# Graph 0's attention ahead of the main loop: score matmuls moved before the transposes, with their results in the lookups' PSUM tiles

## The chip, the cores and the metric

The kernel runs on one core of one Trainium2 chip. The metric is the device time of one execution in microseconds (us); of the kernel before, three runs are given and their median is used. A profile of one further execution comes with its trace.

## What is computed

Sixteen graphs of 1,024 nodes with 128 features pass through four layers, each followed by a residual sum and a layer norm. Layer 0 is a masked attention, layer 1 an edge maximum (`relu` of a sum of two projections, maximum over the neighbours), layer 2 a two-layer perceptron over summed neighbours, layer 3 three graph convolutions over an adjacency thinned row by row ("dilation"). The change lies in layer 0:

```
v = relu(x @ Wv.T + bv);  q = relu(x @ Wq.T + bq);  k = relu(x @ Wk.T + bk)
scores = einsum('bih,bjh->bij', q, k)
h = clip(scores * mask, 0.0, CLAMP_HI) - NEG_PENALTY * (1.0 - mask)
att = softmax(h, axis=2)
out = einsum('bij,bjh->bih', att, v)
x = layernorm(x + out)
```

## The kernel before, in words

**Stages.** After the constants are set up, `layers_012` runs layers 0 to 2 of all graphs together with the dilation. Its main loop is a written order of slots (`slot`, under `tc.manual_schedule`): each slot does one group of layer 1's lookups (matmuls into `pg`, L779, and the maximum on VectorE, L831), and a planner (`advance`) fits the generators of the other work between them, among them the attention of graph b+1. Graph 0's attention cannot hide there, since layer 1 of graph 0 needs its result. So it runs ahead of the loop, by itself. Layer 3 follows after the loop.

**A graph's attention** is two generators that yield where the planner may pause them. `scores(b)` loads the rows of the adjacency, transposes X, makes `qT`, `kT` and `v`, and then goes through eight row blocks t of 128 rows. For each it makes `off` on ScalarE (L320, one buffer: 1 minus the mask), and for each half of 512 columns a score matmul into a PSUM bank `psc` (L329) and a second one that adds the penalty (L330); VectorE clamps the half into `e` and keeps its maximum (L332, `e` has two buffers); `top` joins the two maxima (L336); ScalarE takes the exponential in place and its row sum `total` (L339). `attend(b)` takes one row block's `e`: eight transposes on TensorE in two groups `pe` of four (L367), two copies on ScalarE into `eT` (L370, one buffer), eight products `pav` with `v` in two groups (L377), the reciprocal of the sum (L380), the scaled sum with X into `y` (L381), and the first statistics of the layer norm (L265). After row block 7 the norm's factors are made on GpSimd (L219 to L228), ScalarE writes the normed X (L270), and `scores` goes on with transposes (L278) and the two projections `q` and `p` (L286) that layer 1 starts from.

**PSUM.** `pe`, `pav` and, before the change, `psc` take turns in two banks (`shared`, tag "shared", two buffers). The tag "wide" has two tiles of two banks each; only the lookups' `pg` uses it. The main loop is the only place where `pg` is made.

**Order.** Ahead of the loop a scheduler orders the instructions, from the order in which the program makes them. That order is a loop over t (from L841 on): `front` (`scores(0)`) is run until row block t's `e` is made, and then `back` (`attend(0)`) until it asks for row block t+1. `happened` is a dictionary of marks, by which the generators wait for each other. Each engine has one list of instructions, in the order that results.

Of the kernel before, what the change touches and what calls it, by code (L numbers as in the profile page):

```python
# [29 lines left out]
F32 = mybir.dt.float32  # L30
# [10 lines left out]
P = 128  # L41
T = N // P
# [29 lines left out]
def tile_graph_layers(ctx: ExitStack, tc, a, out):  # L72
# [7 lines left out]
    psum = None  # L80
# [9 lines left out]
    psum = setup.enter_context(tc.tile_pool(name="psum0", bufs=2, space=PSUM))  # L90
# [60 lines left out]
    def four(v):  # L151
        return v.unsqueeze(1).to_broadcast([3, 4, P])
# [83 lines left out]
    def layers_012():  # L236
# [3 lines left out]
        psum = psums.enter_context(tc.tile_pool(name="psumA", bufs=1, space=PSUM))  # L240
# [11 lines left out]
        happened, streams, made = {}, [], []  # L252

        def ask(engine, cost, take=False, give=False, same=False, delay=0.5, after=None, third=False, urgent=False):
            return engine, cost, take, give or urgent and None, 0 if same else delay, after, third

        def shared(name):
            return psum.tile([P, 512], F32, tag="shared", name=name, bufs=2)
# [14 lines left out]
        def columns_of(dst, src, first=0.5):  # L273
            for h in range(2):
                yield ask("PE", 0.44, take=True, delay=0.5 if h else first)
                p = shared("ptr")
                for t in range(4):
                    nc.tensor.transpose(p[:, t * P:(t + 1) * P], src[:, 4 * h + t, :], ident)  # L278
                yield ask("A", 0.59, give=True, same=True)
                nc.scalar.copy(dst[:, halves[h]], p)  # L280

        def product_of(lhsT, rhs, dst, func, bias, delay=0.5):
            for h, s in enumerate(halves):
                yield ask("PE", 0.86, take=True, delay=0.5 if h else delay)
                p = shared("pp")
                nc.tensor.matmul(p, lhsT, rhs[:, s], start=True, stop=True)  # L286
                yield ask("A", 0.6, give=True, same=True)
                if bias is None:
                    nc.scalar.copy(dst[:, s], p)  # L289
                else:  # L290
                    nc.scalar.activation(dst[:, s], p, func, bias=bias)

        def scores(b):

            if b > 1:
                yield ask("Pool", 0, after=("p", b - 1))
            if b > 2:
                yield ask("Pool", 0, after=("rest", b - 3))
            load_rows(b)
            xT = w4.tile([P, N], F32, name="xT")  # L300
            yield from columns_of(xT, X[b])
            qT = w4.tile([P, N], F32, name="qT")
            yield from product_of(WqT, xT, qT, AF.Relu, bq)
            kT = w4.tile([P, N], F32, name="kT")
            yield from product_of(WkT, xT, kT, AF.Relu, bk)
            v = values[b] = w4.tile([P, T, D], F32, name="v")
            for h in range(2):
                yield ask("PE", 1.1, take=True)
                pv = shared("pv").rearrange("p (t d) -> p t d", d=D)
                nc.tensor.matmul(pv, ones_b[:3, :], four(bv3), start=True, stop=False)  # L310
                for t in range(4):
                    nc.tensor.matmul(pv[:, t, :], xT[:, (4 * h + t) * P:(4 * h + t + 1) * P], WvT,
                                     start=False, stop=(t == 3))
                yield ask("A", 0.6, give=True, same=True)
                nc.scalar.activation(v[:, 4 * h:4 * h + 4, :], pv, AF.Relu)
            for t in range(T):

                yield ask("A", 1.05)
                off = w4.tile([P, N], BF, name="off", tag="pen")
                nc.scalar.activation(off, An[b][:, t, :], AF.Identity, bias=ones[:, 0:1], scale=-1.0)  # L320
                if t > 1:
                    yield ask("PE", 0, same=True, after=("back", b, t - 2))
                e = w4.tile([P, N], F32, name="e", bufs=2)

                tops = small.tile([P, 2], F32, name="tops")
                for h, s in enumerate(halves):
                    yield ask("PE", 1.07, take=True)
                    psc = shared("psc")
                    nc.tensor.matmul(psc, qT[:, t * P:(t + 1) * P], kT[:, s], start=True, stop=False)  # L329
                    nc.tensor.matmul(psc, penalty, off[:, s], start=False, stop=True)  # L330
                    yield ask("V", 0.66, give=True)
                    nc.vector.tensor_scalar(e[:, s], psc, CLAMP_HI, None, op0=ALU.min, op1=ALU.max,  # L332
                                            accum_out=tops[:, h:h + 1])
                yield ask("V", 0.1, same=True)
                top = small.tile([P, 1], F32, name="top")
                nc.vector.tensor_scalar(top, tops[:, 0:1], tops[:, 1:2], -1.0, op0=ALU.max, op1=ALU.mult)  # L336
                yield ask("A", 1.1)
                total = small.tile([P, 1], F32, name="total")
                nc.scalar.activation(e, e, AF.Exp, bias=top, accum_out=total)  # L339
                exps[b, t] = e, total  # L340
                happened["e", b, t] = now
            yield ask("A", 0.01, after=("X1", b), delay=0.5)
            xT = w4.tile([P, N], F32, name="xT1", tag="xT")
            yield from columns_of(xT, X[b])
            q = w4.tile([P, NP * PS], F32, name="q", bufs=2)
            nc.gpsimd.memset(q[:, N:], LOWEST)
            yield from product_of(W01[:, 1, :], xT, q[:, :N], None, None)
            qs[b] = q
            happened["q", b] = now
            if b > 1:  # L350
                yield ask("A", 0, same=True, after=("y1", b - 2))
            p = ps[b] = w4.tile([P, N], F32, name="p", bufs=2)
            yield from product_of(Wd, xT, p, AF.Identity, b01)
            happened["p", b] = now

        def attend(b):
            for t in range(T):
                yield ask("PE", 0.01, after=("e", b, t))
                if t == 0:
                    y = w4.tile([P, T, D], F32, name="y0", tag="xT")  # L360
                e, total = exps.pop((b, t))
                eT = w4.tile([P, T, P], F32, name="eT")
                for h in range(2):
                    yield ask("PE", 0.44, take=True, same=(h == 0))
                    p = shared("pe")
                    for c in range(4):
                        nc.tensor.transpose(p[:, c * P:(c + 1) * P],  # L367
                                            e[:, (4 * h + c) * P:(4 * h + c + 1) * P], ident)
                    yield ask("A", 0.59, give=True, same=True)
                    nc.scalar.copy(eT[:, 4 * h:4 * h + 4, :].rearrange("p c i -> p (c i)"), p)  # L370
                happened["back", b, t] = now
                for h in range(2):
                    yield ask("PE", 0.9, take=(h == 0))
                    if h == 0:
                        pav = shared("pav")[:, :D]
                    for c in range(4 * h, 4 * h + 4):
                        nc.tensor.matmul(pav, eT[:, c, :], values[b][:, c, :], start=(c == 0), stop=(c == T - 1))  # L377
                yield ask("V", 0.4, give=True)
                share = small.tile([P, 1], F32, name="share")
                nc.vector.reciprocal(share, total)  # L380
                nc.vector.scalar_tensor_tensor(y[:, t, :], pav, share, X[b][:, t, :], op0=ALU.mult, op1=ALU.add)  # L381
            yield from norm(X[b], y)
            happened["X1", b] = now
# [305 lines left out]
        def load_rows(b):  # L689
            An[b] = apool.tile([P, T, N], F8, name="An", bufs=3)  # L690
            nc.gpsimd.dma_start(out=An[b], in_=adj[b].rearrange("(t p) m -> p t m", p=P))
# [146 lines left out]
        for at in range(2):  # L838
            load_columns(at)
        front, back = scores(0), attend(0)  # L840
        for t in range(T):  # L841
            while ("e", 0, t) not in happened:
                next(front)
            for what in back:
                if what[5] == ("e", 0, t + 1):
                    break
        for _ in front:
            pass
        first = tables_of(0)
# [18 lines left out]
        psum = ctx.enter_context(tc.tile_pool(name="psum", bufs=2, space=PSUM))  # L868
# [301 lines left out]
```

## Time and profile before

| | us |
|---|---|
| median of three runs | 6616.69 |
| the three runs | 6604.93, 6616.69, 6620.51 |
| the profiled execution | 6613.2 |
| its span, first to last instruction | 6611.5 |
| graph 0's row blocks: start of the first transposes to the last L265 | 45.34 to 114.31 |
| start of the transposes of the eight row blocks | 45.34, 54.47, 63.92, 73.58, 81.59, 91.44, 101.09, 108.99 |
| first transpose of layer 1's table (L760) | 128.39 |

Times in the trace count from the first instruction. The profiled execution takes 1.7 us more than its span and lies 3.5 us below the median of the three runs, inside their spread of 15.6 us. Engines are PE (TensorE; PEld its weight loads), DVE (VectorE), ACT (ScalarE), POOL (GpSimd), SP (SyncE). "PEclk" is the share of TensorE's full clock that it was granted. In a line of the timeline the first number is the start, the second the time until the group's last end, and the bracket the idle time of that engine before it and what ended it.

### The profile page before, as it was taken

The numbers are of one execution on the slowest core, as the hardware profiler recorded it, in microseconds if no ns is written. First come the engines' busy times: TensorE is split into PE (matmuls) and PEld (weight loads), VectorE is DVE, ScalarE is ACT, GpSimd is POOL, SyncE is SP. The second block draws the span as 40 slices with busy tenths as digits, with TensorE's granted clock in tenths as the row PEclk, the third lists the DMA queues.
The fourth block names the chain that finished last, engine by engine and source line by source line (L and its number), as shares of the span: only waits on it lengthen the run. The fifth ranks groups of instructions, "written<-read, shape, count | busy, mean of one in ns | idle before, by whom it ended". The sixth has DMA issues, their size and how long they took to land. (4 is left out here: it accounts for less than half of the span.)

```text
span 6611.5 us, 85916 instructions
## 1 busy us (share of the span) xinstructions
PE 5697.7 (86%) x27306; PEld 2883.8 (44%) x27306; DVE 5317.7 (80%) x8130; ACT 3733.9 (56%) x6537; POOL 3844.7 (58%) x11285
## 2 busy tenths in 40 slices
PE   6989898989898989899888898888888768787986
PEld 3434344444444444444444444444443345555643
DVE  3989899999999999999999999999998834444453
ACT  4656566666666666666666656666655523333841
POOL 2675767676767776766666676767676511110126
PEclk8989898989898989898989899999987779888997
DMA  5121212121212121212112212121110156563635
GB/s 37 14 27 22 30 24 36 20 27 26 28 28 27 27 27 26 28 26 31 28 29 30 27 26 27 26 27 28 25 25 9 32 93 120 105 124 102 230 128 166
DMA packets 478381, 317.02 MB, mean 48 GB/s; under 512 B 301162, under 2 KB 429668, under 8 KB 473828
## 3 DMA queue, kind: packets, MB, share of 16 engines
q0 software_dynamic: 105648, 84.20, 14.6%
q1 hardware_dynamic: 367600, 226.13, 11.7%
q8 instruction: 214, 3.51, 0.2%
q10 hardware_dynamic: 4676, 1.19, 0.1%
q14 instruction: 243, 1.99, 0.1%
HBM read 412.71 MB, written 117.18 MB: 80 GB/s over the span
## 5 line engine op out<-in xcount | busy, mean ns | idle before, releaser
L831 DVE TENSOR_TENSOR best<-best,pg 128x1024 f32<-128x1024 f32 x2720 | 3234.4, 1210 | 309.0 <-PE pg L779 300.5
L749 ACT ACTIVATE hot<-pm,one_less 128x512 fp32r<-128x512 f32 x2752 | 1882.3, 688 | 1115.1 <-PE pm L748 1102.9
L779 PE MATMUL pg<-hot,high 64*128 64x512 f32 x5504 | 1479.1, 534 | 453.6 <-DVE best L831 417.8
L779 PE MATMUL pg<-hot,low 64*128 64x512 f32 x5504 | 1173.3, 423 | 0.0
L748 PE MATMUL pm<-AT,lit 120*128 120x512 fp8e4 x2752 | 1143.8, 416 | 9.3 <-ACT hot L749 6.2
L779 PEld LDWEIGHTS pg<-hot,high 64*128 64x128 f32 x5504 | 547.9, 196 | 1265.1 <-DVE best L831 792.4
L616 POOL TENSOR_SCALAR sc<-low_counts,half_mask,rest 16x1 f32<-16x1 f32 x992 | 435.7, 439 | 399.6 <-DVE rest L603 305.8
L779 PEld LDWEIGHTS pg<-hot,low 64*128 64x128 f32 x5504 | 573.4, 205 | 0.0
L748 PEld LDWEIGHTS <-lit 120*128 120x128 fp8e4 x2752 | 274.5, 100 | 624.8 <-issue 560.8
L621 POOL TENSOR_SCALAR sc<-sc 16x1 f32<-16x1 f32 x992 | 430.1, 434 | 105.0
L770 ACT CAST low<-pt 128x256 fp32r<-128x256 f32 x688 | 255.6, 371 | 396.3 <-PE pt L768 392.1
L980 POOL TENSOR_TENSOR length<-length,mhalf 128x8 f32<-128x8 f32 x48 | 78.9, 1644 | 571.7 <-DVE length L979 571.7
L618 POOL TENSOR_SCALAR sc<-sc 16x1 f32<-16x1 f32 x992 | 341.8, 345 | 107.7
L624 POOL TENSOR_SCALAR last_rank<-V,sc 16x31 f32<-16x31 bf16 (+30 forms) x992 | 387.1, 390 | 0.0
L623 POOL TENSOR_SCALAR hit<-V,sc 16x31 bf16<-16x31 bf16 (+30 forms) x992 | 372.5, 376 | 0.0
L768 PE MATMUL pt<-high,less 128*128 128x256 f32 x688 | 303.2, 441 | 66.3 <-ACT high L763 58.9
L467 DVE TENSOR_TENSOR sub<-sub,q 128x24 f32<-128x24 f32 (+11 forms) x768 | 306.6, 400 | 24.6 <-ACT q L289 10.5
L619 POOL TENSOR_SCALAR sc<-sc 16x1 f32<-16x1 f32 x992 | 270.1, 272 | 83.3
L937 ACT CAST m<-near 128x1024 fp32r<-128x1024 fp8e4 x256 | 253.3, 1044 | 112.7 <-DVE near L906 59.8
L760 PE MATMUL pt<-ident,sub 128*128 128x128 f32 x1376 | 293.9, 298 | 24.7 <-ACT hot L749 22.0
L377 PE MATMUL pav<-v,eT 128*128 128x128 f32 x2048 | 307.6, 296 | 2.1 <-ACT eT L370 2.1
L617 POOL TENSOR_SCALAR sc<-sc 16x1 f32<-16x1 f32 x992 | 256.6, 259 | 86.6
(258 smaller groups left out, 9495.7 us busy)
## 6 DMA issues: line engine op xcount, KB each, us to landing
removed<-gone SPq DMA_DIRECT2D x128, 256.0 KB
An<-in_adj_dram POOLq DMA_DIRECT2D x16, 1024.0 KB, 15.1
E<-in_adj_dram POOLq DMA_DIRECT2D x128, 128.0 KB, 6.8
gone_all<-removed POOLq DMA_DIRECT2D x64, 256.0 KB, 12.1
near<-in_adjT_dram POOLq DMA_DIRECT2D x16, 1024.0 KB, 17.3
h<-x SPq DMA_DIRECT2D x32, 512.0 KB
kept<-near SPq DMA_DIRECT2D x16, 1024.0 KB
share<-share SPq DMA_DIRECT2D x32, 512.0 KB
```

Source lines behind the costliest of these rows:

```text
L377: nc.tensor.matmul(pav, eT[:, c, :], values[b][:, c, :], start=(c == 0), stop=(c == T - 1))
L467: nc.vector.tensor_max(sub[:, :n_g, n:2 * n], sub[:, :n_g, 0:n], qg[:, 2 * g0:2 * g0 + n_g, k:k + 1].to_broadcast([P, n_g, n]))
L616: gp.tensor_scalar(half, mine, half_mask[:, m], rest[:, n:n + 1], op0=ALU.mult, op1=ALU.add)
L618: gp.tensor_scalar(sf, half, 5.5, sf, op0=ALU.is_gt, op1=ALU.mult)
L621: gp.tensor_scalar(to, at, sf, none, op0=ALU.subtract, op1=ALU.subtract)
L623: gp.tensor_scalar(hit[:, n, n + 1:], V[:, n, n + 1:], at, None, op0=ALU.is_equal)
L624: gp.tensor_scalar(last[:, n + 1:], V[:, n, n + 1:], to, None, op0=ALU.is_le)
L748: nc.tensor.matmul(pm, lit[:, r, :], AT[b * (T + 1) + c][:, halves[h]], start=True, stop=True)
L749: nc.scalar.activation(hots[s][:, halves[h]], pm, AF.Relu, bias=one_less)
L768: nc.tensor.matmul(pt, less, high, start=False, stop=True, skip_group_check=True)
L779: nc.tensor.matmul(pg[:, a], part[rows, at * P:(at + 1) * P], hots[s][rows, halves[h]], start=(k == 0), stop=(k == 1))
L831: nc.vector.tensor_max(own, own, pg)
```

## The change

The loop over t runs `attend` one row block later than `scores`: `scores(0)` makes row block t+1 before `attend(0)` takes row block t, and a ninth turn takes the last. Until the mark `planned` is set, ahead of the main loop, `psc` is no longer a bank of the pair "shared": each half takes a "wide" tile of two banks, and uses the bank of its own half. The first half's tiles and the second half's thus take turns in the two "wide" tiles, so each half has one bank. In the main loop `psc` is taken as before.

```
@@ -325,7 +325,10 @@
                 tops = small.tile([P, 2], F32, name="tops")
                 for h, s in enumerate(halves):
                     yield ask("PE", 1.07, take=True)
-                    psc = shared("psc")
+                    if "planned" in happened:
+                        psc = shared("psc")
+                    else:
+                        psc = psum.tile([P, 2, 512], F32, tag="wide", name="psc", bufs=2)[:, h]
                     nc.tensor.matmul(psc, qT[:, t * P:(t + 1) * P], kT[:, s], start=True, stop=False)
                     nc.tensor.matmul(psc, penalty, off[:, s], start=False, stop=True)
                     yield ask("V", 0.66, give=True)
@@ -838,12 +841,14 @@
         for at in range(2):
             load_columns(at)
         front, back = scores(0), attend(0)
-        for t in range(T):
-            while ("e", 0, t) not in happened:
+        for t in range(T + 1):
+            while t < T and ("e", 0, t) not in happened:
                 next(front)
-            for what in back:
-                if what[5] == ("e", 0, t + 1):
-                    break
+            if t:
+                for what in back:
+                    if what[5] == ("e", 0, t):
+                        break
+        happened["planned"] = 0
         for _ in front:
             pass
```

## The prediction

> **What bounds the kernel now.** I read the page first, then the stretch of graph 0's attention: a table of windows, its waits, the timeline of one row block. The page:
>
> ```profile
> span 6611.5 us, 85916 instructions
> PE 5697.7 (86%) x27306; PEld 2883.8 (44%) x27306; DVE 5317.7 (80%) x8130; ACT 3733.9 (56%) x6537; POOL 3844.7 (58%) x11285
> PEclk8989898989898989898989899999987779888997
> ```
>
> No engine is full over the span, but that is a mean over stages. The change touches one stage, 45 to 114 us of 6611.5, so 1% of the span; the whole question is what happens there and whether the rest simply starts earlier. Windows (stretch, its length, each engine's busy us, then granted clock, DMA share, GB/s):
>
> ```profile
> core 0: us, PE busy (x) PEld busy (x) DVE busy (x) ACT busy (x) POOL busy (x), PEclk, DMA share, GB/s
> 63.90:73.50 9.60, 6.93 (x30) 5.02 (x30) 2.41 (x8) 3.33 (x5) 0.00 (x0) 0.82 0.00 0
> 73.50:81.60 8.10, 5.30 (x31) 3.52 (x31) 2.45 (x9) 3.37 (x6) 0.00 (x0) 1.00 0.00 0
> 129.00:200.00 71.00, 63.54 (x319) 31.06 (x319) 53.31 (x85) 49.81 (x92) 48.77 (x174) 0.95 0.04 5
> ```
>
> The first two rows are one row block each. The busy times add up to hardly more than the length (5.30 + 2.45 + 3.37 = 11.1 of 8.10 us), where the main loop (last row) has 167 us of PE, DVE and ACT in 71: in the attention the engines work by turns. The same row block takes 9.6 or 8.1 us with the granted clock, 0.82 or 1.00. DMA moves nothing there. The waits of the stretch 41 to 119 us (engine and line, whom it waited for, us in total, times, longest) say who stands for whom:
>
> ```profile
> DVE y L381 <- PE pav L377: 35.2, 8, 4.9
> ACT off L320 <- PE psc L330: 30.0, 6, 5.7
> DVE e L332 <- PE psc L330: 21.3, 15, 15.7
> PE pe L367 <- ACT e L339: 19.7, 8, 2.7
> ```
>
> TensorE waits 2.4 us per row block for the exponential before it may transpose; all others wait for TensorE. One row block at full clock:
>
> ```profile
> 73.58 1.09 PE L367 MATMUL pe<-ident,e 128*128 128x128 f32 x8 [2.43 <-ACT e L339]
> 74.32 1.07 ACT L370 COPY eT<-pe 128x512 f32<-128x512 f32 x2 [0.80 <-PE pe L367]
> 74.96 2.05 PE L377 MATMUL pav<-v,eT 128*128 128x128 f32 x16 [0.29 <-ACT eT L370]
> 76.85 1.02 PE L329 MATMUL psc<-kT,qT 128*128 128x512 f32 x2
> 77.05 0.35 DVE L381 SCALAR_TENSOR_TENSOR y<-pav,share,X 128x128 f32<-128x128 f32 x1 [3.33 <-PE pav L377]
> 77.71 0.38 PE L330 MATMUL psc<-off,penalty 128*128 128x512 bf16 x1
> 77.92 1.02 PE L329 MATMUL psc<-kT,qT 128*128 128x512 f32 x2
> 78.78 0.38 PE L330 MATMUL psc<-off,penalty 128*128 128x512 bf16 x1
> 79.20 0.69 DVE L332 TENSOR_SCALAR_CACHE_REDUCE e<-psc 128x512 f32<-128x512 f32 x1 [0.38 <-PE psc L330]
> 79.26 1.15 ACT L320 ACTIVATE off<-An,ones 128x1024 bf16<-128x1024 fp8e4 x1 [3.87 <-PE psc L330]
> 79.93 0.21 DVE L336 TENSOR_SCALAR top<-tops 128x1 f32<-128x1 f32 x1
> 80.31 1.13 ACT L339 ACTIVATE e<-e,top 128x1024 f32<-128x1024 f32 x1
> 81.59 0.66 PE L367 MATMUL pe<-ident,e 128*128 128x128 f32 x4 [2.43 <-ACT e L339]
> ```
>
> Read it as one chain: transposes, copy, products, the next row block's scores, clamp, maximum, exponential, transposes again. From 73.58 to 81.59 nothing overlaps it. From the first transposes (45.34) to the eighth (108.99) that makes 63.65 / 7 = 9.09 us per row block.
>
> [...]by windows of 1 us the clock is 0.50 from 38.7 to 48.7 us, after TensorE had stood idle from 36 us on, and again in 55.7 to 58.6, 65.9 to 69.1, 82.9 to 86.1, 93.0 to 96.3 and 110.5 to 113.2; 24 to 36 us, without a gap, is at 1.00. So the idle 2.4 us per row block costs twice. [...]before, five results per row block share two banks.
>
> **The change, part by part.** *No instruction is added or taken away.* With both programs built, GpSimd's and SyncE's instructions stand in the same order, so no DMA is moved past another. TensorE's order differs over one run of 154 instructions, VectorE's over 43, ScalarE's over 24, all inside the eight row blocks; from the layer norm on, the order is the same. `psc` leaves the pair "shared" for 16 tiles, an even number, so the later banks fall as before; `pg` first needs the "wide" tiles long after. These parts cost nothing.
>
> *The moved order.* TensorE, for row block k: 4+4 transposes(k), first score half of k+2, first four products(k), its penalty, second score half of k+2, last four products(k), its penalty. ScalarE: off(k+2), first copy(k), exponential(k+1), second copy(k). VectorE: first clamp of k+1, y(k-1), second clamp of k+1, statistics, top(k+1), reciprocal(k+1). I count from S, the start of the second penalty of row block k+1, all steps from the timeline above, at full clock:
> - off(k+2) has one buffer and waits for this penalty: S+0.48 (78.78 to 79.26), and the next on ScalarE 1.05 later (79.26 to 80.31): S+1.53. This is the step with a new queue: the first copy(k) stands behind off(k+2) though its transposes are ready at S+0.95 (0.21 penalty, 0.74 from transposes to copy), and the products wait for that.
> - first copy(k) S+1.53, products may start 0.64 later (74.32 to 74.96): S+2.17. TensorE until then: penalty 0.21, transposes at most 1.09, score half 0.86 (76.85 to 77.71): S+2.16. Both come together.
> - four products 0.945 (half of 74.96 to 76.85), penalty 0.21, score half 0.86: S+4.18. Last four products need the second copy, which stands behind exponential(k+1): y at S+0.20 takes 0.35, clamp to top 0.73, statistics 0.29, 0.25 from top to the exponential (107.44 to 107.69 in another row block): S+1.82, while ScalarE is free at S+2.07; the exponential with its sum takes 1.22, the copy starts at S+3.29, and products may start at S+3.93, before 4.18. Hidden by 0.25 us; beyond that every delay of it counts.
> - last four products 0.945: next S at S+5.13.
> So 5.13 us per row block, TensorE busy nearly throughout (sum 1.09 + 1.72 + 0.42 + 1.89 = 5.12), against 8.0 at full clock before: 2.9 us from overlap, and on average 1.1 from the clock that no longer falls.
>
> *Start.* Penalty of row block 0 at 41.83 and its first clamp until 43.14 stay. Score halves of row block 1 then take twice 0.86 at half clock: 43.15 to 44.87, and on. The clock changes seen lie on a grid of 3.4 us (38.7, 48.7, so one at 45.3); [...]I take full clock from there: second half done at 45.95, S0 = 46.16. If it comes only at 48.7, about 1.0 us is lost. *End.* S6 = 46.16 + 6 x 5.13 = 76.94. Then no off and no scores are left: copies at +0.95 and +1.49, exponential(7) +2.03 to +3.25, products(6) to +3.48, transposes(7), copy +4.22, products +4.86 to +6.75, y +6.95, statistics +7.33: 84.3. Before: 114.31. **Gain 30.0 us.** What is late next is the GpSimd norm and the half-clock projections up to 128.39, unchanged.
>
> *Does it reach the end?* The order after is the same, the DMA that runs at 1.1 of its share up to 60 us (adjacency, E) ends before 84 too, and nothing waits for the clock on the wall. I take the shift whole: 6613.2 - 30.0 = 6583.2 for the profiled execution (1.7 us outside its span kept), and 6616.69 - 30.0 = **6586.7** for the median, 0.45%. Unknown costs: late clock +1.0; handoffs in the new order, not in the trace before, from 0 (a gain is excluded, since TensorE's 5.1 binds) to 0.4 per row block, the margin of the exponential plus as much again: 0 to 2.4, taken at 0. The median itself moves by about 8 us, half the runs' spread.
>
> **Rivals.**
> 1. *The clock still falls in part.* [...]windows with 57% kept full clock before (96.7 to 100.1), which speaks against. Were half of the rows at half rate (2 x 4.9 = 9.8 us), the mean is 7.5 and the gain 30.0 - 6 x 2.35 = 16: 6601. Were all of them, the start, six cycles and the end give about 118 us against 114.31: slightly lost, 6620.
> 2. *The main loop loses it (slower).* The mean clock 0.904 means some 19% of 6611 / 3.41 = 1,939 windows at half rate, about 370. The earlier start shifts the loop on that grid; a window that turns cold costs at most half, 1.7 us. From 18 more cold windows on the kernel is slower than before; 30 more give 6616.7 - 30 + 51 = 6638. Against it: three runs that start anywhere on the grid differ by 15.6 us, nine windows.
> 3. *The change doesn't do what it says.* Each half has one bank, not two; were the clamp late, scores would wait. The clamp of k+1's first half is read before S, the second by S+1.2, the scores want them at S+1.3 and S+3.3: free. A wrong order is excluded by the built programs.
>
> **How the numbers follow.** Forecast 0.83; rival 1 0.12, of which most lies within the bound; rival 2 0.04; rival 3 0.01. About 0.3%, 20 us, is what a measurement of this kernel can tell from no change. Gain 26.6 to 30.0 and 8 us of the median up and down give 6579 to 6598; widened to 6574 and 6602 to take in rival 1's half. Faster 0.84, same 0.12, slower 0.04.
>
> **What would show it.** Right: transposes of successive row blocks 5.1 us apart; clock 1.00 from about 45 to 84 us; last L265 near 84; first L760 near 98; later differences of the same size. Wrong: waits of the products for the copies over 0.3 us per row block (ScalarE's order binds), clock 0.50 in the stretch, or a main loop that is longer than before by ten us or more.

## The result and the profile after

| | before | after |
|---|---|---|
| median | 6616.69 (five runs, 6604.93 to 6620.51) | 6580.25 (five runs, 6577.91 to 6583.07) |
| ratio | | 0.9953 [0.994, 0.9965] |
| profiled execution, and its span | 6613.2, 6611.5 | 6583.07, 6581.4 |
| mean granted clock over the span | 0.904 | 0.906 |
| first transposes of the eight row blocks | 45.34 ... 108.99 | 47.17, 52.32, 57.43, 62.54, 67.65, 72.76, 77.87, 81.09 |
| last L265 of graph 0 | 114.31 | 84.90 |
| first transpose of layer 1's table | 128.39 (L760) | 98.98 (L763) |

The kernel is 36.4 us faster by its medians, against 30.0 forecast, and 30.1 us faster by its two profiled spans. Of these 30.1 us, 29.4 are there at the first table transpose, ahead of the main loop. Behind it the lead of one profile over another wanders by several us (last table of the next section), so the close agreement of 30.1 with 29.4 is in part chance. In the changed file the lines move by three: L367 is L370, L377 is L380, L381 is L384.

The page hardly changes, as one per cent of the span can't show in it:

```profile
span 6581.4 us, 85782 instructions
PE 5669.1 (86%) x27177; PEld 2870.4 (44%) x27306; DVE 5314.9 (81%) x8130; ACT 3735.2 (57%) x6537; POOL 3854.6 (59%) x11285
PEclk9899899999898989898989899999998788888998
```

The 129 fewer PE instructions than before are records that this trace lacks: e5, the same kernel, has 27306 again.

The windows of the stage do (the columns are those of before: stretch, length, busy us of each engine, then clock, DMA share, GB/s). The first row is the start, the next three are one row block each, the fifth is the stage at full clock:

```profile
core 0: us, PE busy (x) PEld busy (x) DVE busy (x) ACT busy (x) POOL busy (x), PEclk, DMA share, GB/s
42.00:47.17 5.17, 4.43 (x7) 1.71 (x7) 1.70 (x6) 2.82 (x4) 0.00 (x0) 0.50 1.12 106
47.17:52.32 5.15, 5.15 (x31) 3.90 (x30) 2.25 (x10) 3.24 (x5) 1.22 (x3) 0.95 1.12 105
52.32:57.43 5.11, 5.03 (x30) 3.63 (x30) 2.14 (x9) 3.23 (x5) 0.00 (x0) 1.00 1.12 109
57.43:62.54 5.11, 5.09 (x31) 3.63 (x30) 2.14 (x9) 3.24 (x5) 0.00 (x0) 1.00 0.57 53
48.00:84.00 36.00, 35.36 (x220) 26.23 (x222) 14.18 (x55) 22.28 (x36) 1.22 (x3) 1.00 0.38 36
```

A row block has the same instructions as before and takes 5.11 us instead of 7.9 to 9.9. TensorE is busy 5.03 to 5.15 us of it: it has become the bound of the stage, and the other engines work beside it (5.09 + 2.14 + 3.24 = 10.5 of 5.11 us). The clock is at 1.00 from 47.7 us on, which is 0.5 us into the first row block. The third and fourth rows show one more thing: a DMA share of 1.12 in the early row blocks does not lengthen them (5.11 us with 1.12 and with 0.57). The waits of 41 to 89 us:

```profile
DVE e L335 <- PE psc L333: 19.1, 2, 15.7
DVE share L383 <- ACT e L342: 12.4, 7, 1.8
ACT off L320 <- PE psc L333: 12.0, 6, 2.6
DVE y L384 <- PE pav L380: 9.2, 8, 2.5
PE pav L380 <- ACT eT L373: 0.3, 1, 0.3
```

The line "PE pe <- ACT e", 19.7 us before, is gone: TensorE no longer waits for the exponential. What is left of long waits stands on engines that have time. (The 19.1 us of the clamp are the wait for the first scores, 15.7 once, and one more.) One row block of the timeline, from one second penalty to the next:

```profile
52.11 0.38 PE L333 MATMUL psc<-off,penalty 128*128 128x512 bf16 x1
52.32 1.05 PE L370 MATMUL pe<-ident,e 128*128 128x128 f32 x8
52.58 1.15 ACT L320 ACTIVATE off<-An,ones 128x1024 bf16<-128x1024 fp8e4 x1 [1.87 <-PE psc L333]
53.21 1.02 PE L332 MATMUL psc<-kT,qT 128*128 128x512 f32 x2
53.64 0.57 ACT L373 COPY eT<-pe 128x512 f32<-128x512 f32 x1
54.11 1.15 ACT L342 ACTIVATE e<-e,top 128x1024 f32<-128x1024 f32 x1
54.26 1.16 PE L380 MATMUL pav<-v,eT 128*128 128x128 f32 x8
55.25 0.57 ACT L373 COPY eT<-pe 128x512 f32<-128x512 f32 x1
55.47 1.02 PE L332 MATMUL psc<-kT,qT 128*128 128x512 f32 x2
56.33 1.05 PE L380 MATMUL pav<-v,eT 128*128 128x128 f32 x8
57.22 0.38 PE L333 MATMUL psc<-off,penalty 128*128 128x512 bf16 x1
```

Three row blocks are in work at once: `off` and the score halves belong to row block k+2, the exponential to k+1, transposes, copies and products to k. (The first score half's penalty has no record in this block; its weight load stands at 55.14, and in the next block the penalty itself is at 60.36. The halves' matmuls of a group are x2, since one 512-column product in f32 is two matmuls here.)

### The profile page after: what moved, and what is told of

It reads as the page before. It is cut to its first block, busy times and chain, and to the rows that moved or that the text cites. A ratio compares the mean times of both kernels' runs of the same rounds, so it can differ in the third digit from the quotient of the medians.

```text
span 6581.4 us, 85782 instructions
## 1 busy us (share of the span) xinstructions
PE 5669.1 (86%) x27177; PEld 2870.4 (44%) x27306; DVE 5314.9 (81%) x8130; ACT 3735.2 (57%) x6537; POOL 3854.6 (59%) x11285
## 5 line engine op out<-in xcount | busy, mean ns | idle before, releaser
L470 DVE TENSOR_TENSOR sub<-sub,q 128x24 f32<-128x24 f32 (+11 forms) x768 | 306.6, 400 | 24.7 <-ACT q L289 10.5
L763 PE MATMUL pt<-ident,sub 128*128 128x128 f32 x1376 | 292.7, 297 | 24.4 <-ACT hot L752 21.1
L380 PE MATMUL pav<-v,eT 128*128 128x128 f32 x2048 | 302.6, 292 | 0.5 <-ACT eT L373 0.3
```

The source lines that it names most:

```text
L470: nc.vector.tensor_max(sub[:, :n_g, n:2 * n], sub[:, :n_g, 0:n], qg[:, 2 * g0:2 * g0 + n_g, k:k + 1].to_broadcast([P, n_g, n]))
```

## The experiments

Each ran beside the kernel before on the same chip. "Row block" is the distance of successive first transposes, "table" the first table transpose. All of before's results in this section are medians of 9 to 25 runs; "less" is what a run's median lies below that of the kernel before beside it.

| run | edit | row block | last L265 | table | median | less | ratio [95%] |
|---|---|---|---|---|---|---|---|
| e1 | before, with the banks alone | 10.6 per two | 86.4 | 100.53 | 6587.81 | 29.8 | 0.9955 [0.9938, 0.9971] |
| e2 | after, with the order alone | 7.1 | 99.3 | 113.43 | 6596.84 | 20.8 | 0.9967 [0.9955, 0.9978] |
| e3 | after, both halves in one tile | 6.0 | 91.6 | 105.68 | 6587.66 | 29.9 | 0.9959 [0.9944, 0.9974] |
| e4 | before, unused matmuls added | 8.1 | 108.3 | 122.34 | 6607.71 | 9.9 | 0.9986 [0.9979, 0.9992] |
| e5 | after, again | 5.11 | 84.8 | 98.99 | 6581.55 | 34.3 | 0.9948 [0.9935, 0.996] |
| e6 | before, again | 7.9 to 9.9 | 114.3 | 128.38 | 6619.77, one run | | |
| e7 | after, two buffers for off | 5.05 | 83.8 | 97.94 | 6578.27 | 37.6 | 0.9943 [0.9928, 0.9958] |
| e8 | after, rows of the adjacency first | 5.11 | 83.0 | 97.07 | 6582.14 | 33.7 | 0.9946 [0.9934, 0.9959] |
| e9 | e8 with its order mended | 5.11 | 77.2 | 91.55 | 6582.72 | 36.5 | 0.9945 [0.9931, 0.9958] |
| e10 | before, a third time | 8.0 to 10.6 | 113.9 | 128.02 | 6619.43, one run | | |
| e11 | e9 and e7 | 5.05 | 76.9 | 91.63 | 6580.83 | 42.7 | 0.9936 [0.9923, 0.9948] |
| e12 | after, beside e11 | 5.11 | 84.7 | 98.83 | 6587.48 | 36.0 | 0.995 [0.9936, 0.9963] |

The theory: TensorE's idle time goes, because the scores of row block k+2 fill it; that needs the order and the banks. Rivals: the banks do it alone; the order does it alone; only the clock does it.

**e1: the banks alone.** The kernel before with only the `psc` lines of the change (`psum.tile(..., tag="wide", bufs=2)[:, h]` until `planned` is set); the loop over t as before.

> Only the banks of the scores change; the loop over the row blocks stays as before. Mine: what the change gains is that the next scores need no bank of the pair; the scheduler then moves them ahead by itself. Its list for TensorE takes the scores of two row blocks between two pairs of products, and I count 10.4 us for two row blocks, so 5.2 to 5.5 each, TensorE's clock at 1.00, the last L265 at 85 to 88 us, and 27 to 30 us less than before in all. Rival: the written order of the loop is what counts; then row blocks stay at 7 us or more and the gain is under 15 us.

Two row blocks of its timeline:

```profile
58.12 1.09 PE L370 MATMUL pe<-ident,e 128*128 128x128 f32 x8
59.04 1.02 PE L332 MATMUL psc<-kT,qT 128*128 128x512 f32 x2
59.90 2.01 PE L380 MATMUL pav<-v,eT 128*128 128x128 f32 x16
61.76 0.60 PE L370 MATMUL pe<-ident,e 128*128 128x128 f32 x4
62.41 0.61 PE L370 MATMUL pe<-ident,e 128*128 128x128 f32 x4
63.09 2.05 PE L380 MATMUL pav<-v,eT 128*128 128x128 f32 x16
64.97 3.16 PE L332 MATMUL psc<-kT,qT 128*128 128x512 f32 x6
67.31 1.13 ACT L342 ACTIVATE e<-e,top 128x1024 f32<-128x1024 f32 x1
68.58 0.66 PE L370 MATMUL pe<-ident,e 128*128 128x128 f32 x4
```

Freed from the shared banks, the scheduler itself moves scores ahead, in pairs: of four score halves one goes ahead of the products of two row blocks (59.04), and three follow them (64.97). These two row blocks take 10.46 us (58.12 to 68.58), and 10.6 on average over the stage, so 5.2 to 5.3 each, hardly more than after. By the table the banks alone are worth 128.39 - 100.53 = 27.9 of the change's 29.4 us. So the theory that order and banks are both needed does not hold: the first rival very nearly does, and the loop's new order adds 1.5 us to it. (Its full clock came 0.9 us earlier than after's, at 46.8 instead of 47.7; at a granted clock of 0.50 that length loses some 0.5, an estimate from the two times.)

**e2: the order alone.** After, with one line: `psc = shared("psc")` always.

> Only the loop's order changes; scores, transposes and products share two banks as before. Mine: the transposes of a row block wait until the scores ahead are clamped out of their bank, and both copies stand behind the exponential: S+1.82 to +3.04, products +3.68 to +5.57, two score halves to +7.5. So 7.5 us per row block (8.0 at full clock before), the last L265 near 98, and 13 to 17 us less than before, most of it from a clock that stays up. Rival: the order alone does it; 5.1 us per row block and 30 us less.

```profile
78.35 0.66 PE L367 MATMUL pe<-ident,e 128*128 128x128 f32 x4 [0.35 <-DVE e L332]
78.71 1.13 ACT L339 ACTIVATE e<-e,top 128x1024 f32<-128x1024 f32 x1
79.84 1.05 ACT L370 COPY eT<-pe 128x512 f32<-128x512 f32 x2
80.45 2.05 PE L377 MATMUL pav<-v,eT 128*128 128x128 f32 x16 [1.45 <-ACT eT L370]
82.34 1.02 PE L329 MATMUL psc<-kT,qT 128*128 128x512 f32 x2
83.42 1.02 PE L329 MATMUL psc<-kT,qT 128*128 128x512 f32 x2
```

With two banks for `pe`, `pav` and `psc` the scores follow the products (82.34 after 80.45), the second group of transposes waits 0.35 us until a score half is clamped out of its bank, and the copies stand behind the next exponential: TensorE waits 1.45 us for `eT`. A row block takes 7.1 us (one of them 8.76, since the clock fell once, from 65.4 to 68.8), and 15.0 us are gained by the table. So 27.9 and 15.0 are not shares of a sum: each part alone removes much of the same idle time.

**e3: four banks, taken in another way.** After, but both halves of a row block lie in one tile, so that the two tiles alternate by row block:

```
+                        if h == 0:
+                            both = psum.tile([P, 2, 512], F32, tag="wide", name="psc", bufs=2)
+                        psc = both[:, h]
```

> As the changed kernel, but both halves of a row block lie in one two-bank tile, so all four banks are used and a row block's scores need not wait for the clamp of the row block before. The scheduler's list for ScalarE then has both copies behind the exponential. Mine: the place of the copies decides, not the banks: exponential S+1.82 to +3.04, products from +3.68, 6.4 us per row block, the last L265 near 92, 22 us less than before and 8 more than the changed kernel. Rival: more banks are as good or better; 5.1 us or less per row block and 30 us less than before.

```profile
66.93 1.04 PE L372 MATMUL pe<-ident,e 128*128 128x128 f32 x8
68.24 1.13 ACT L344 ACTIVATE e<-e,top 128x1024 f32<-128x1024 f32 x1
69.37 1.05 ACT L375 COPY eT<-pe 128x512 f32<-128x512 f32 x2
69.99 2.05 PE L382 MATMUL pav<-v,eT 128*128 128x128 f32 x16 [0.76 <-ACT eT L375]
72.95 1.04 PE L372 MATMUL pe<-ident,e 128*128 128x128 f32 x8
```

6.02 us per row block (66.93 to 72.95): more banks in use than after, and slower by 0.9. The scheduler's order is another one: both copies stand behind the exponential (68.24, then 69.37), and the products wait 0.76 for them. In the changed kernel the first copy goes ahead of it (53.64 before 54.11). That wait is most of the 0.9 us. So more banks alone don't help; the order that they lead to counts as well. (e7 below has both copies behind the exponential too, without a wait, so the place of the copies is not enough by itself either.) By its median e3 is as far below before as e1, 29.9 and 29.8 us with four runs each; only the landmarks of the stage, 22.7 and 27.9 us earlier, tell the two apart.

**e4: the clock alone.** The kernel before, with six more 512-column matmuls per row block from the second on (and one of one column, so that they wait for `top`) in the time in which TensorE waits for the exponential; their result is not used.

```
+                if "planned" not in happened and t:
+                    fill = psum.tile([P, 2, 512], F32, tag="wide", name="fill", bufs=2)[:, 0]
+                    nc.tensor.matmul(fill[:, 0:1], ident, peaks[t], start=True, stop=True)
+                    for i in range(6):
+                        nc.tensor.matmul(fill, ident_b, An[b][:, t, 0:512], start=True, stop=True)
```

> The kernel before, with six more 512-column matmuls per row block on TensorE (their results unused) while it waits for the exponential. Nothing else moves. Mine: part of the gain is the clock that no longer falls: all row blocks take 8.0 to 8.2 us (9.09 on average before), clock 1.00 from the second row block on, the last L265 near 106, and 7 to 8 us less than before though work is added. Rival: the slow row blocks have another cause; they stay at 9.6 us and the time is the same or, if the added matmuls delay the transposes, up to 7 x 1.3 = 9 us longer.

```profile
51.00:110.00 59.00, 47.33 (x263) 29.97 (x264) 17.47 (x58) 22.44 (x34) 2.23 (x10) 1.00 0.18 17
```

The clock stays at 1.00 from 50.6 us on, and a row block takes 8.1 us: work that computes nothing brings 6.05 us (128.39 to 122.34). It is what the prediction called the clock's part, 1.1 us in each of seven row blocks, less what the first one lost at half rate until 50.6. The rest of the change's 29.4, some 23 us, is put down to overlap; it is a difference and was not measured by itself.

**e5 and e6: both kernels again**, unchanged.

> The changed kernel once more, with more rounds. Its trace starts layer 1 (first L763) 29.4 us earlier than the kernel before and ends 30.1 us earlier, but the medians lay 36 us apart. Mine: the attention's 29 to 30 us are shifted whole to the end, the other 6 are scatter of the long part behind it: the medians come to 28 to 34 us apart. Rival: the earlier start also shortens the main loop; the medians stay 35 us or more apart.

> The kernel before, profiled once more. Mine: row blocks take about 8.0 us where the clock holds and about 9.7 where it falls, but which of them do is not the same as in the first profile[...]; the first L763 of layer 1 falls within 125 to 132 us. Rival: the same row blocks are slow again, each within 0.1 us, so the pattern belongs to the program.

The stage repeats to 0.1 us: 98.99 and 128.38 against 98.98 and 128.39. The medians are 34.3 apart (6615.83 before).

**e7: a second buffer for `off`.** After, with every second row block's `off` in another tag. It tests what it costs that `off` stands ahead of the first copy in ScalarE's queue.

```
-                off = w4.tile([P, N], BF, name="off", tag="pen")
+                off = w4.tile([P, N], BF, name="off", tag="pen" if "planned" in happened or t % 2 == 0 else "parts")
```

> The changed kernel, with every second row block's off (1 minus the mask) in a buffer that lies idle then, so that off need not wait for the penalty before it and the first copy no longer stands behind it. Mine: per row block only TensorE's sum is left, 4.9 us against the 5.11 measured, at most 1.3 us in all, which the time cannot show; where the scheduler writes another order for the first row blocks they may lose as much. Rival: ScalarE's order is the real bound and TensorE's 5.1 a coincidence; row blocks fall to 4.5 us or less and the last L265 comes 4 us earlier or more.

```profile
57.59 1.02 PE L332 MATMUL psc<-kT,qT 128*128 128x512 f32 x2
57.97 1.13 ACT L342 ACTIVATE e<-e,top 128x1024 f32<-128x1024 f32 x1
58.45 0.38 PE L333 MATMUL psc<-off,penalty 128*128 128x512 bf16 x1
58.66 1.02 PE L332 MATMUL psc<-kT,qT 128*128 128x512 f32 x2
59.10 1.05 ACT L373 COPY eT<-pe 128x512 f32<-128x512 f32 x2
59.72 2.05 PE L380 MATMUL pav<-v,eT 128*128 128x128 f32 x16
```

With `off` made a row block early, both score halves go ahead of the products, and the copies may stand behind the exponential without a wait: no bracket on the products. In the steady state a row block takes 5.05 us, and TensorE is busy for all of it (5.05 us in 61.82 to 66.87; its expectation had put this sum at 4.9); the table comes 1.04 us earlier.

**e8 and e9: an earlier start.** The first row block waits for the arrival of the adjacency's rows (`off` at 40.17, [6.75 <-DMA An]). e8 loads these rows ahead of the columns AT and of the `half_rows`, with the halving of `half_rows` moved to the start of the dilation:

```
         load_x(0)
+        front, back = scores(0), attend(0)
+        next(front)
         for at in range(2):
             load_columns(at)
-        front, back = scores(0), attend(0)
+        for b in range(B):
+            q, g = divmod(b, G)
+            nc.gpsimd.dma_start(out=half_rows[g * R:(g + 1) * R, :, q],
+                                in_=a["nodemask"][b].rearrange("(k r) -> r k", r=R))
```

> The changed kernel, with graph 0's adjacency rows loaded ahead of the columns and of thirteen of the sixteen small node mask loads; the mask's halving moves to the start of the dilation. Mine: what is late first now is that load: off of row block 0 waits for it until 40.2 us, and TensorE's clock falls meanwhile. It would land near 32, before the first scores are done; first transposes near 39 against 47.17, last L265 near 77, clock 1.00 throughout, and 7 to 8 us less than the changed kernel. Rival: the transfers share the bandwidth, so that the rows land hardly earlier or X later; 2 us or less are gained.

That failed. The rows were there at 32.3, but the scheduler put this `off` on ScalarE ahead of the copy `qT`, which then stood behind it until 33.3, and layer 1's first products, which need AT until 33.9, ahead of the projections on TensorE. The first transposes came at 45.54 and the table 1.9 us earlier: the work that was to profit had been queued behind the load. e9 adds an order without waits, `off` behind the last `v` and layer 1's first products behind the projections:

```
+                if "planned" not in happened and t == 0:
+                    behind(filled, start_at)
...
+                    if s == -2:
+                        behind(projected, start_at)
```

> The changed kernel with the rows of graph 0's adjacency loaded first, its copy `off` of row block 0 behind the projections of v on ScalarE, and layer 1's first products behind the projections of q and k on TensorE; the halving of the half_rows at the start of the dilation. Theory (the first row block waited only for the arrival of An, the rest of the stage is a chain of fixed length behind it, and a shift of it reaches the end whole): off of row block 0 at 32 to 33 us instead of 40.2, first transposes near 38 to 39 instead of 47.17, last L265 near 76 to 77 instead of 84.9, first table transpose near 90 to 92 instead of 98.98, median 7 to 9 us below the changed kernel, near 6573. Rival A (the later stage then waits for something of fixed time, such as AT, the half_rows or the weights): last L265 near 77 but first table transpose not before 95, median within 4 us of the changed kernel. Rival B (the earlier attention runs while the clock is still cold or the loads slow it): row blocks over 5.5 us apart, last L265 after 80.

```profile
32.38 1.15 ACT L317 ACTIVATE off<-An,ones 128x1024 bf16<-128x1024 fp8e4 x1 [3.15 <-DMA An<-in_adj_dram]
39.39 1.28 PE L369 MATMUL pe<-ident,e 128*128 128x128 f32 x8
91.55 0.44 PE L763 MATMUL pt<-ident,sub 128*128 128x128 f32 x2 [0.92 <-ACT hot L752]
```

First transposes at 39.39 instead of 47.17, last L265 at 77.2 and the table at 91.55, 7.4 us earlier, all as expected. But the median, 6582.72, is not 7 us lower: against the kernel before beside it (6619.18) it is 36.5 us less, where the changed kernel had 36.4 and 34.3.

**e10: before, once more.** In e6 the clock's changes had fallen on the same moments as in the first profile, so that it could not tell whether the stage's length depends on them.

> The kernel before once more, one look, for the 5 to 6 us between the difference of the medians (36.4 and 34.3 us) and the shift of the first table transpose (29.4 us). If the length of its attention depends on where the clock's changes fall on their grid of 3.4 us, its first table transpose lies anywhere between 123 (every row block at full clock, 8.0 us) and 133 us in an execution of another phase, and not at 128.4 as twice before; if the phase plays no part, it lies at 128.4 again whatever the phase, and the 5 to 6 us are of the long part behind it.

Here the clock rises at 51.15 and stays up to 64.81; in the first profile it was up from 48.63 to 55.46 and from 58.87 to 65.70. Other row blocks are slow (the first two take 10.55 and 8.0 us, where they took 9.13 and 9.45), and the table comes at 128.02. So the stage has this length in another phase too: the 5 to 7 us that the medians differ by beyond the 29.4 do not come from it. They lie behind the table.

**e11 and e12: does an earlier start come through?** Both edits of e7 and e9 in one kernel, and the changed kernel beside it on the same chip.

> Both edits of e9 and e7 in one: the rows of the adjacency first, with off of row blocks 0 and 1 behind the projections of v, and every second off of the stage in a buffer of its own. First table transpose: 91.55 of e9 less the 1.0 that the second buffer gave in e7, so about 90.5, 8.5 us ahead of the changed kernel's 98.98. Theory A (e9's earlier start is kept, and its profiled loss of 7 us between graph 5 and the end, and its median, were scatter of the executions): median 7 to 9 us below the changed kernel of the same call, near 6573, and the lead over the changed kernel held to the end in the profile within 5 us. Theory B (an earlier start beyond the change's own is given back later, in a loop whose order is the same): median within 3 us of the changed kernel of the same call.

> The changed kernel once more, as the partner of e11 on the same chip. From its two measurements so far: median 6578 to 6584, first table transpose at 99.0. If it is 34 to 36 us below the kernel before again, the difference between the medians is 5 to 6 us more than the shift of the first table transpose in three of three measurements.

e11's table comes at 91.63, not 90.5: with e9's start the second buffer saved 0.3 us at the last L265 and nothing at the table. Its median is 6.65 us below e12's (7.2 by the table), and its span, 6575.9, is 9.5, 5.5 and 1.1 us below those of the three profiles of the changed kernel (6585.4, 6581.4, 6577.0). That is nearer to the first theory, that e9's missing gain is scatter; but e9's own five runs don't show the gain, and the intervals of e9 and e11 overlap, so it is not settled. Of all the kernels run, e11 has the lowest ratio. e12 is 36.0 us below the kernel before (6623.52).

**Where the lead goes.** One landmark per row, us by which each profile is ahead of the first profile of before (whose time is in the second column). The landmarks are the first `off` of a graph's attention, and layer 3's first matmul:

| landmark | before at | e6 | e10 | after | e5 | e12 | e7 | e9 | e11 |
|---|---|---|---|---|---|---|---|---|---|
| first table transpose | 128.4 | 0.0 | 0.4 | 29.4 | 29.4 | 29.6 | 30.5 | 36.8 | 36.8 |
| third graph | 470.4 | 1.8 | 2.5 | 33.7 | 31.9 | 33.4 | 33.0 | 38.8 | 38.8 |
| seventh graph | 1762.4 | 0.1 | -1.3 | 32.0 | 35.8 | 28.4 | 35.0 | 37.7 | 39.1 |
| eighth graph | 2083.1 | 0.2 | -3.8 | 29.2 | 34.6 | 24.1 | 33.6 | 32.6 | 39.2 |
| twelfth graph | 3369.3 | 0.5 | -6.6 | 27.5 | 32.8 | 25.0 | 40.7 | 33.4 | 36.4 |
| last graph | 4668.9 | 0.2 | -5.5 | 32.6 | 36.7 | 31.9 | 44.7 | 30.4 | 39.2 |
| layer 3 | 5332.7 | -2.8 | -6.2 | 32.0 | 36.2 | 31.6 | 44.2 | 29.8 | 36.3 |
| end of the span | 6611.5 | -6.6 | -6.2 | 30.1 | 34.5 | 26.1 | 43.2 | 28.3 | 35.6 |

Behind the table each engine's order is the same in all of these (but for the halving of `half_rows` in e9 and e11), yet the lead of one profile wanders: e12, the same kernel as after, loses 8 us between the third and the twelfth graph, finds 7 of them again by the last and then loses 6, e7 wins 14 that nothing in its edit explains, e9 loses 5 in one graph. The five profiles that the table leaves out wander too, from 27.9, 15.0, 22.7, 6.1 and 31.3 us at the table (e1 to e4, e8) to 21.2, 15.9, 27.7, -4.1 and 26.2 at the end. From the eighth to the last graph, e7's stretch and then e9's (windows of each):

```profile
2049.50:4624.20 2574.70, 2300.65 (x11272) 1106.11 (x11271) 2378.58 (x3558) 1603.10 (x2961) 1835.48 (x5454) 0.92 0.19 27
```

```profile
2050.50:4638.50 2588.00, 2316.30 (x11272) 1113.23 (x11270) 2380.09 (x3557) 1603.47 (x2962) 1836.53 (x5454) 0.91 0.19 27
```

The same instructions; VectorE and ScalarE are busy for the same time within 1.6 us, TensorE 15.65 us longer, the stretch 13.3 us longer. So in this pair the wandering comes with TensorE's rate. It isn't the mean clock alone: in the graph where e9 lost 5 us (325.8 us at 0.92, before 320.7 at 0.93), e11 took 320.6 at 0.91. Whether it matters where in a graph the clock is low, and not only for how long, was not followed further.

## Why the prediction was right, point by point

- **The row block's cycle**, 5.13 forecast, is 5.11, and its steps lie where they were put. From S = 52.11: `off` at +0.47 (forecast 0.48), first copy +1.53 (1.53), products +2.15 (2.17), exponential +2.00 (2.07), second copy +3.14 (3.29), last products +4.22 (4.18), next S +5.11 (5.13). Durations from the trace before held in the new order to 0.15 us. The unknown cost of handoffs, put between 0 and 0.4 per row block and taken at 0 without a measurement, was 0: in e7, without `off` ahead of the copy, the cycle is 5.05, so 0.06 is all that ScalarE's new queue costs.
- **The start** is the one mis-sized term. Full clock was assumed from 45.3; it came at 47.7, since the clock's changes fell on other moments in this execution. TensorE was busy for 2.12 us from 40.87 to 44.28 (one more penalty has no record) and throughout from 44.28 to 47.70, both at 0.50, and the clock rose at the end of the second stretch. First transposes at 47.17 put S0 at 46.96 (0.21 before, as at 52.11 and 52.32), not 46.16. The prediction had 1.0 for this case; the adjacency's rows landed 0.46 earlier, which gives part of it back and was luck.
- **The end** from S6 = 77.66 to the last L265 took 7.24 us, forecast 7.4. The sum: 84.90 against 84.3; table 98.98 against "near 98".
- **The clock**: 1.00 from 47.7 to 88.7, so rival 1 (it falls in part) did not come. The spacing of 3.4 us that the prediction saw in the trace before is there again: all 231 changes of the granted clock on record in before, and all 223 in after, lie a whole multiple of 3.413 us behind the first one (88.66 - 47.70 = 40.96 = 12 x 3.413 in after; 48.63, 55.46, 58.87, 65.70, 69.11 in before). Which moments these are differs from execution to execution (the stage's first rise at 48.63 in before, at 51.15 in e10), which is why 45.3 could not be had from the trace before. The clock also fell after stretches that were not wholly idle: between 48.63 and 113.48 of the first profile, of the stretches of 3.413 us at 1.00, it fell after those in which TensorE was busy for 0.29 to 0.44 of the time, and stayed after those with 0.55 or more. That does not hold throughout: in the main loop of the same profile it also fell after 1335.46 to 1338.87, with 0.65 (2.22 us).
- **What raises the clock** was not shown; full clock from 45.3 was the author's estimate. In before the clock rose at 48.63 after 3.41 us with TensorE busy for 3.29, of which transposes (L367) took 1.97 and products 1.50, partly at once. It did not rise at 123.72 after 3.42 us with 3.28 of transposes (L278) and projections (L286), only at 127.14, after 3.42 us busy throughout. What transposes do for it by themselves stays open.
- **A wrong reading.** The prediction has the clock at 1.00 from 24 to 36 us. The trace has no record of the clock before 28.15, which the windows show as 1.00, and the matmuls ran at half rate until then: those with 128x512 f32 results started 0.85 us apart at 26.5 (1.06 us for one) and 0.43 apart from 28.2 (0.59 for one). Its sum does not use this.
- **The banks**: rival 3 feared that one bank per half would make the scores wait. There is no such wait in the steady state, and e1 shows that the banks are the larger part: 27.9 of 29.4 us come without the moved order of the loop, along which the prediction counts its steps. It did not weigh the two parts against each other. e3's number, 6.0 us with more banks in use, shows that the order must fit as well.
- **The shift reaches the end whole**: 29.4 us at the table, 30.1, 34.5 and 26.1 at the end of three profiles of after against the first of before, which was the shortest of its three (e6 and e10 end 6.6 and 6.2 us later). Rival 2 (the loop loses it) did not come; its some 370 stretches at half rate are 374 of 3.413 us at 0.50 in the record of before.
- **The median** fell by 36.4, 34.3 and 36.0 us in three comparisons, not by 30.0. The prediction gave the median's own scatter as 8 us, and so its time of 6586.7 is 6.4 us too high within its range. The other edits show such a surplus of the median over the shift of the table as well, 1.9 to 7.2 us in e1 to e4, e7, e8 and e11, and only e9 does not. Over all runs on record the means of before (57 runs) and after (15) lie 34.3 us apart, 31 to 37 by their scatter (an estimate), where the table has 29.4: so it is not scatter alone. e10 shows only that the surplus isn't in graph 0's attention. Its cause stays open.

## What to carry to other kernels

When the engines of a stage work by turns, add up TensorE's own busy time per step: if it is far below the step's length, work of the next step but one can fill the gap, provided that its results have banks of their own and that the copies in ScalarE's queue don't make the products wait; count both before counting the gain. Try the banks alone first: here the scheduler then found an order by itself that was worth 27.9 of 29.4 us. An idle gap of a third of a step (2.4 of 8.0 us) also let the clock fall here, and that cost was a fifth of the gain (e4: 6.05 of 29.4 us). This stage ahead of a long loop passed its gain on, but a gain below some 7 us could not be read from the total of five runs (e9), only from the landmark at the end of its own stage; with 20 runs beside 25, e4's 6 us showed.

## What the runs showed of the hardware that was not expected

- In the traces of before and after, all changes of the granted clock (231 and 223) lie a whole multiple of 3.413 us behind the first one, and the moments differ between executions: the first rise of the stage lay at 48.63, 48.65 and 51.15 in before, e6 and e10, one kernel, and at 47.70, 46.92 and 47.52 us in after, e5 and e12, another. In after, the scores that started at 42.74 stayed at a clock of 0.50 past 44.28, one such moment, until 47.70, the next.
- Identically ordered work in the main loop took 2574.7 us in one execution (e7) and 2588.0 in another (e9), with TensorE busy 15.7 us longer, while VectorE's and ScalarE's busy times stayed the same within 1.6 us.
- In 52 to 57 us the DMA share was 1.12 and 109 GB/s were moved, and the row block took 5.11 us as with 0.57: the loads cost this row block nothing.
